# A depthwise convolution accumulated in PSUM, one-bank PSUM tiles in the frequency stage, and TensorE in written order

## The chip, the cores and the metric

The kernel runs on one core of a Trainium2 chip. The metric is device time in microseconds (us) for one execution, the median of several; the profile is of one execution. TensorE is called PE in the profile (its weight loads PEld), VectorE DVE, ScalarE ACT, GpSimd POOL, and the DMA queues of SyncE SP. SBUF is the on-chip working memory; PSUM is the memory that TensorE writes to, eight banks of 512 f32 values in each of 128 partitions.

## The reference

Eight images of 128 x 128 pixels and 64 channels, all f32, go through two layers. The first is criss-cross attention (every pixel attends to its row and its column). The second, called the mixer here, is what the change is about:

```python
h  = _pw(_ln(x, g1, b1), w_te, b_te)                  # 64 -> 128 channels at each pixel
F  = jnp.fft.fft2(h.astype(jnp.complex64), axes=(1, 2))
fr = jnp.concatenate([jnp.real(F), jnp.imag(F)], axis=-1)
fc = jax.nn.gelu(_pw(fr, w_fc, b_fc), approximate=False)   # 256 -> 256
re, im = (fc[..., :HID], fc[..., HID:])
sp = jnp.real(jnp.fft.ifft2(re + 1j * im, axes=(1, 2)))
x1 = x + _pw(sp, w_tp, b_tp)                          # 128 -> 64
h2 = _pw(_ln(x1, g2, b2), w_fe, b_fe)                 # 64 -> 128
d  = lax.conv_general_dilated(h2, w_dw, window_strides=(1, 1), padding='SAME',
         dimension_numbers=('NHWC', 'HWIO', 'NHWC'), feature_group_count=HID) + b_dw   # 3 x 3, depthwise
d  = jax.nn.gelu(d, approximate=False)
return x1 + _pw(d, w_fp, b_fp)                        # 128 -> 64
```

## The kernel before

The attention layer runs first for all eight images and leaves its result in DRAM (`x2`). The mixer then has, for each image, two stages written as Python generators. `fourier(b)` is the frequency stage: Fourier transforms along both axes as matmuls with tables, the 256 x 256 channel mix with its gelu (`fcps`, `gl`), and the inverse (`yps`, `dps`), added to `x1`. `mlp(b)` is what follows: normalisation, expansion to 128 channels, the 3 x 3 convolution, gelu, and the last matmul. The MLP of image b-1 is woven into the frequency stage of image b, piece by piece; the last MLP runs by itself.

PSUM before: `ps_f` two tiles of two banks, `ps_m` and `ps_c` two tiles of one bank each, eight banks in all.

```python
W_STEP, K_STEP, I_STEP = 2.0, 7.0, 5.0
PIECES = 5
LEAD = 6
# ... cut ...
        ps_f = ctx.enter_context(tc.tile_pool(name="m_psf", bufs=2, space=PSUM))
        ps_m = ctx.enter_context(tc.tile_pool(name="m_psm", bufs=2, space=PSUM))
        ps_c = ctx.enter_context(tc.tile_pool(name="m_psc", bufs=2, space=PSUM))
# ... cut: fourier, one of 8 steps of the first transform ...
                aps = ps_f.tile([P, 8, P], F32, tag="fc", name="aps")
                for c in range(8):
                    nc.tensor.matmul(aps[:, c, :], lhsT=xn[:, c0 + c, :], rhs=fwd, start=True, stop=True)
                nc.scalar.copy(at[:, :, c0 : c0 + 8], aps.rearrange("p c k -> p k c"))
                yield W_STEP
# ... cut: the channel mix of one group of four frequencies ...
                    for half in range(2):
                        ps = ps_f.tile([P, 2, 512], F32, tag="fc", name="fcps")
                        cols = slice(half * HID, half * HID + HID)
                        for sgn, w in enumerate((wplus, wminus)):
                            mean = gg[0] == 0
                            nc.tensor.matmul(ps[:, sgn, 0:n], lhsT=w[:, cols], rhs=fv, start=True, stop=not mean)
# ... cut ...
                        nc.scalar.activation(gl[:, :, 0:n], ps[:, :, 0:n], AF.Gelu, bias=bfc[:, half : half + 1])
                        nc.gpsimd.tensor_tensor(
                            gl[:, 0, 0:n], gl[:, 0, 0:n], gl[:, 1, 0:n], ALU.add if half == 0 else ALU.subtract
                        )
# ... cut: the end of the inverse transform ...
        def inverse_w(xs, c0, ys):
            dps = ps_f.tile([P, 8, P], F32, tag="fc", name="dps")
            for g in range(2):
                nc.tensor.matmul(
                    dps[:, 4 * g : 4 * g + 4, :].rearrange("p c h -> p (c h)"), lhsT=idw,
                    rhs=ys[:, 4 * g : 4 * g + 4, :].rearrange("p c h -> p (c h)"), start=True, stop=True,
                )
            for s in range(2):
                xv = xs[s][:, :, c0 : c0 + 8]
                nc.vector.tensor_tensor(xv, dps[:, :, 64 * s : 64 * s + 64].rearrange("p c h -> p h c"), xv, ALU.add)
```

The MLP works on 16 chunks `k` of 8 rows. `normed` (POOL) scales the rows (`xc`), `transposed` brings channels to the partitions (`tpn` on PE, `xtn` on ACT), `expand` makes `h2` (two `hp` matmuls on the two halves of the partitions, and ACT), `taps` is the convolution, `gelu`, `shrink` the last matmul (`op`) and `store` the addition and the DMA:

```python
            def expand(k):
                # ... cut: h2, its borders (POOL memsets), two rows taken over from the chunk before ...
                hps = [ps_c.tile([P, 4, P], F32, tag="mc", name="hp") for _ in range(2)]
                for s in range(2):
                    half = slice(64 * s, 64 * s + 64)
                    nc.tensor.matmul(
                        hps[s].rearrange("p j w -> p (j w)"), lhsT=wfe[half, :],
                        rhs=xt[half, :, :].rearrange("p j w -> p (j w)"), start=True, stop=True,
                    )
                # ... cut: two ACT instructions, hps to h2 ...

            def taps(k, lo, hi):
                i0, i1 = span(k)
                if lo == 0:
                    accs[k] = p2.tile([P, CH + 1, P], F32, tag="acc", name="acc")
                av = accs[k][:, 0 : i1 - i0, :]
                for t in range(lo, hi):
                    src = h2s[k][:, i0 + t // 3 : i1 + t // 3, t % 3 : t % 3 + P]
                    if t == 0:
                        nc.scalar.activation(av, src, AF.Identity, bias=bdw, scale=wdw[:, 0:1])
                    else:
                        nc.vector.scalar_tensor_tensor(
                            out=av, in0=src, scalar=wdw[:, t : t + 1], in1=av, op0=ALU.mult, op1=ALU.add
                        )

            def gelu(k):
                i0, i1 = span(k)
                av = accs[k][:, 0 : i1 - i0, :]
                nc.scalar.activation(av, av, AF.Gelu)
            # ... cut ...
            for k in range(n_ch):
                if k > 0:
                    gelu(k - 1)
                if k + 1 < n_ch:
                    transposed(k + 1)
                if k == 4:
                    statistics(1)
                taps(k, 1, 3)
                yield
                held = shrink(k - 1, 0) if k > 0 else None
                taps(k, 3, 5)
                yield
                if held:
                    store(*held)
                taps(k, 5, 6)
                yield
                if k + 1 < n_ch:
                    expand(k + 1)
                if k + 2 < n_ch:
                    normed(k + 2)
                taps(k, 6, 8)
                yield
                if k + 1 < n_ch:
                    taps(k + 1, 0, 1)
                taps(k, 8, 9)
                yield
```

In the attention layer four engines keep the order in which the program is written. In the mixer the compile-time scheduler orders every engine's instructions itself, before the program ever runs.

## Time and profile before

| | us |
|---|---|
| median of 3 runs | 3831.16 (3825.0 to 3836.74) |
| span of the profiled execution | 3833.7 |

| engine | busy us | share of the span | instructions |
|---|---|---|---|
| PE | 3370.7 | 88% | 33046 |
| PE weight loads | 2387.3 | 62% | 33046 |
| DVE | 2676.3 | 70% | 4432 |
| ACT | 1741.7 | 45% | 2341 |
| POOL | 1607.0 | 42% | 1347 |

An f32 matmul appears as two records. In the slices of the page each digit is the busy share of a fortieth of the span in tenths, and the PEclk row is the clock that TensorE was granted, in tenths of full speed. In a row of a group stand the line, the engine, the operation, output and inputs by the program's names, shapes and the number of instructions; then busy us and mean ns of one; then how long the engine stood idle just before them and who ended that wait. A line of the waits has who waited for whom, the us in total, the number of times and the longest. Busy time counts overlapping records once.

### The profile page before, as it was taken

The numbers are of one execution on the slowest core, as the hardware profiler recorded it, in microseconds if no ns is written. First come the engines' busy times: TensorE is split into PE (matmuls) and PEld (weight loads), VectorE is DVE, ScalarE is ACT, GpSimd is POOL, SyncE is SP. The second block draws the span as 40 slices with busy tenths as digits, with TensorE's granted clock in tenths as the row PEclk, the third lists the DMA queues.
The fourth block names the chain that finished last, engine by engine and source line by source line (L and its number), as shares of the span: only waits on it lengthen the run. The fifth ranks groups of instructions, "written<-read, shape, count | busy, mean of one in ns | idle before, by whom it ended". The sixth has DMA issues, their size and how long they took to land.

```text
span 3833.7 us, 79138 instructions
## 1 busy us (share of the span) xinstructions
PE 3370.7 (88%) x33046; PEld 2387.3 (62%) x33046; DVE 2676.3 (70%) x4432; ACT 1741.7 (45%) x2341; POOL 1607.0 (42%) x1347
## 2 busy tenths in 40 slices
PE   7989989899998679998998998998998998999454
PEld 4666666666666457666665666666665665666333
DVE  3556565664665500788888987888988988978867
ACT  3544535435353233453553553553553554554222
POOL 0333243332433534356356356356356356253111
PEclk7989889999897889998998998998998998999555
DMA  4534434354342511012112112112112112100000
GB/s 101 128 94 121 109 98 124 93 129 108 91 119 69 170 44 45 6 39 58 37 39 58 37 39 58 37 39 58 37 39 58 37 39 53 37 17 17 12 19 20
DMA packets 505190, 242.94 MB, mean 63 GB/s; under 512 B 417026, under 2 KB 486018, under 8 KB 502786
## 3 DMA queue, kind: packets, MB, share of 16 engines
q1 hardware_dynamic: 504834, 237.90, 23.1%
q8 instruction: 260, 4.26, 0.5%
q14 instruction: 96, 0.79, 0.1%
HBM read 169.13 MB, written 67.63 MB: 62 GB/s over the span
## 4 chain that ended last, share of the span: by engine, by line
PE 52%; DVE 26%; issue 8%; POOL 6%; ACT 4%; DMA 2%; SPq 1%; DVEq 0%; POOLq 0%; ACTq 0%
DVE acc L748 18%; PE e L202 6%; PE op L770 5%; PE fcps L595 5%; PE hp L724 4%; PE zp L265 3%; PE yps L655 3%; PE dps L663 3%; PE yps L649 3%; PE sp L289 3%; PE pq L183 3%; PE zp L278 3%; POOL xn L542 2%; PE gps L622 2%; DVE negH L211 2%
## 5 line engine op out<-in xcount | busy, mean ns | idle before, releaser
L748 DVE SCALAR_TENSOR_TENSOR acc<-h,wdw,acc 128x1024 f32<-128x1024 f32 (+2 forms) x1024 | 1612.1, 1594 | 151.5 <-ACT acc L746 131.2
L602 POOL TENSOR_TENSOR gl<-gl 128x512 f32<-128x512 f32 (+2 forms) x272 | 487.1, 1796 | 454.0 <-ACT gl L601 453.9
L770 PE MATMUL op<-wfp,acc 128*128 128x64 f32 x2048 | 292.0, 304 | 163.7 <-ACT acc L755 162.8
L770 PEld LDWEIGHTS op<-wfp,acc 128*128 128x128 f32 x2048 | 278.2, 218 | 187.9 <-ACT acc L755 180.0
L601 ACT ACTIVATE gl<-fcps,bfc 128x1024 f32<-128x1024 f32 (+2 forms) x272 | 292.5, 1077 | 190.7 <-PE fcps L595 180.9
L765 POOL TENSOR_TENSOR ot<-x,bfp 128x512 f32<-128x512 f32 (+1 forms) x144 | 226.2, 1576 | 358.9 <-DMA out_dram<-ot 321.8
L243 ACT ACTIVATE att<-e 128x1024 f32<-128x1024 f32 x256 | 248.3, 1022 | 242.9 <-PE e L202 242.8
L339 POOL TENSOR_TENSOR yo<-yo,xb 128x512 f32<-128x512 f32 x128 | 161.0, 1280 | 430.4 <-issue 296.3
L245 POOL TENSOR_SCALAR_AFFINE_SELECT att<-att 128x1024 f32<-128x1024 f32 x128 | 136.8, 1093 | 419.6 <-ACT att L243 419.6
L729 ACT ACTIVATE h<-hp,bfe 128x512 f32<-128x512 f32 x256 | 171.4, 688 | 291.3 <-PE hp L724 291.1
L595 PE MATMUL fcps<-f,wplus 128*128 128x512 f32 (+2 forms) x544 | 293.7, 622 | 0.0
L622 PEld LDWEIGHTS gps<-wtp,gl 128*128 128x128 f32 x2016 | 246.0, 193 | 57.7 <-issue 55.2
L595 PE MATMUL fcps<-f,wminus 128*128 128x512 f32 (+2 forms) x544 | 275.9, 589 | 0.0
L669 DVE TENSOR_TENSOR x<-dps,x 128x512 f32<-128x512 f32 x128 | 86.2, 683 | 265.2 <-PE dps L663 265.2
L542 POOL TENSOR_TENSOR xn<-xl,scale 128x512 f32<-128x512 f32 x128 | 238.4, 1873 | 57.1 <-DMA xl<-x 56.9
L724 PE MATMUL hp<-xtn,wfe 64*128 64x512 f32 x512 | 243.6, 739 | 21.1 <-DVE ot L774 19.8
L755 ACT ACTIVATE acc<-acc 128x1024 f32<-128x1024 f32 (+2 forms) x128 | 135.4, 1058 | 258.6 <-DVE acc L748 258.6
L202 PE MATMUL e<-qkH 8*128 8x128 f32 (+1 forms) x4096 | 199.7, 316 | 54.4 <-DVE negH L211 50.3
L694 POOL TENSOR_TENSOR xc<-x,scale 128x512 f32<-128x512 f32 x128 | 189.1, 1482 | 129.2 <-PE tpn L703 88.2
L622 PE MATMUL gps<-wtp,gl 128*128 128x64 f32 x2016 | 241.1, 273 | 0.9 <-POOL gl L602 0.9
L202 PEld LDWEIGHTS e<-qkH 8*128 8x128 f32 (+1 forms) x4096 | 164.3, 212 | 122.1 <-DVE negH L211 60.0
L202 PEld LDWEIGHTS e<-qkW 8*128 8x128 f32 (+1 forms) x4096 | 140.6, 194 | 126.4 <-DVE negW L211 36.0
(138 smaller groups left out, 6389.1 us busy)
## 6 DMA issues: line engine op xcount, KB each, us to landing
xl<-in_x_dram SPq DMA_DIRECT2D x256, 128.0 KB
xh<-in_x_dram SPq DMA_DIRECT2D x64, 512.0 KB
xw<-in_x_dram SPq DMA_DIRECT2D x256, 128.0 KB
x<-yo SPq DMA_DIRECT2D x256, 128.0 KB
xl<-x SPq DMA_DIRECT2D x128, 256.0 KB
x<-x SPq DMA_DIRECT2D x16, 2048.0 KB
out_dram<-ot SPq DMA_DIRECT2D x120, 256.0 KB
qkH<-joint SPq DMA_DIRECT2D x256, 2.0 KB
```

Of the source, the lines that this page charges most:

```text
L202: nc.tensor.matmul(es[q // 2][:, q % 2, i, :], lhsT=qk[part, lhs, 4 * (r % 2) + i, :], rhs=qk[part, rhs, 4 * (r % 2) + i, :], start=True, ...
L243: nc.scalar.activation(att, e.rearrange("p q i w -> p (q i) w"), AF.Exp)
L542: nc.gpsimd.tensor_tensor(xn[:, :, h : h + NORM_ROWS], xl.rearrange("p h c -> p c h"), scale1[:, b, h : h + NORM_ROWS].unsqueeze(1).to_bro ...
L595: nc.tensor.matmul(ps[:, sgn, 0:n], lhsT=w[:, cols], rhs=fv, start=True, stop=not mean)
L601: nc.scalar.activation(gl[:, :, 0:n], ps[:, :, 0:n], AF.Gelu, bias=bfc[:, half : half + 1])
L602: nc.gpsimd.tensor_tensor(gl[:, 0, 0:n], gl[:, 0, 0:n], gl[:, 1, 0:n], ALU.add if half == 0 else ALU.subtract)
L622: nc.tensor.matmul(gps[:, j, t, :], lhsT=src[:, 0, j * P : j * P + P], rhs=wtp, start=True, stop=True)
L694: nc.gpsimd.tensor_tensor(xc, rows, scale[:, k * CH : k * CH + CH].unsqueeze(2).to_broadcast([P, CH, C]), ALU.mult)
L724: nc.tensor.matmul(hps[s].rearrange("p j w -> p (j w)"), lhsT=wfe[half, :], rhs=xt[half, :, :].rearrange("p j w -> p (j w)"), start=True, ...
L748: nc.vector.scalar_tensor_tensor(out=av, in0=src, scalar=wdw[:, t : t + 1], in1=av, op0=ALU.mult, op1=ALU.add)
L765: nc.gpsimd.tensor_tensor(ot[:, o : o + m, :], rows, bfp.unsqueeze(1).to_broadcast([P, m, C]), ALU.add)
L770: nc.tensor.matmul(op[:, i, :], lhsT=accs[k][:, a + i, :], rhs=wfp, start=True, stop=True)
```

## The change

Five things are changed together, all in the mixer:

- The convolution's sum `acc` moves from SBUF to PSUM (`ps_a`, two tiles of one bank), in parts of at most four rows; the gelu reads PSUM and writes a new SBUF tile `gd`. The aim is to take the sum's traffic out of SBUF, and with a part per bank to let one part's first tap or gelu run beside the other part's taps.
- That needs two banks, so `ps_f` shrinks to two tiles of one bank: `aps`, `fcps` and `dps` are cut into halves, each with its own evacuation.
- TensorE keeps the written order in the mixer too; the other engines are still ordered by the scheduler.
- The MLP's pieces are put into another order: `shrink` and `store` come later in the chunk, and the second half's statistics are spread over four chunks.
- The step weights that weave MLP pieces into the frequency stage follow the halved `aps` step.

```diff
@@ -35,7 +35,7 @@
 CH = 8
 NORM_ROWS = 8
 
-W_STEP, K_STEP, I_STEP = 2.0, 7.0, 5.0
+W_STEP, K_STEP, I_STEP = 1.0, 7.0, 5.0
 PIECES = 5
 LEAD = 6
 
@@ -441,6 +441,7 @@
         ps_f = ctx.enter_context(tc.tile_pool(name="m_psf", bufs=2, space=PSUM))
         ps_m = ctx.enter_context(tc.tile_pool(name="m_psm", bufs=2, space=PSUM))
         ps_c = ctx.enter_context(tc.tile_pool(name="m_psc", bufs=2, space=PSUM))
+        ps_a = ctx.enter_context(tc.tile_pool(name="m_psa", bufs=2, space=PSUM))
 
         ident = const.tile([P, P], F32, tag="ident", name="m_ident")
         make_identity(nc, ident)
@@ -552,11 +553,11 @@
             im = images[b]
             xn = im["xn"]
             at = big.tile([P, P, C], F32, tag="big", name="at")
-            for c0 in range(0, C, 8):
-                aps = ps_f.tile([P, 8, P], F32, tag="fc", name="aps")
-                for c in range(8):
+            for c0 in range(0, C, 4):
+                aps = ps_f.tile([P, 4, P], F32, tag="fc", name="aps")
+                for c in range(4):
                     nc.tensor.matmul(aps[:, c, :], lhsT=xn[:, c0 + c, :], rhs=fwd, start=True, stop=True)
-                nc.scalar.copy(at[:, :, c0 : c0 + 8], aps.rearrange("p c k -> p k c"))
+                nc.scalar.copy(at[:, :, c0 : c0 + 4], aps.rearrange("p c k -> p k c"))
                 yield W_STEP
             gt = big.tile([P, C, 2, 64], F32, tag="big", name="gt")
             pend_fc, pend_tp = None, None
@@ -588,17 +589,17 @@
                     fv = f.rearrange("p k h -> p (k h)")[:, 0:n]
                     gs = []
                     for half in range(2):
-                        ps = ps_f.tile([P, 2, 512], F32, tag="fc", name="fcps")
+                        gl = p2.tile([P, 2, 512], F32, tag="gl%d" % half, name="gl")
                         cols = slice(half * HID, half * HID + HID)
                         for sgn, w in enumerate((wplus, wminus)):
+                            ps = ps_f.tile([P, 512], F32, tag="fc", name="fcps")
                             mean = gg[0] == 0
-                            nc.tensor.matmul(ps[:, sgn, 0:n], lhsT=w[:, cols], rhs=fv, start=True, stop=not mean)
+                            nc.tensor.matmul(ps[:, 0:n], lhsT=w[:, cols], rhs=fv, start=True, stop=not mean)
                             if mean:
                                 nc.tensor.matmul(
-                                    ps[:, sgn, 0:1], lhsT=dc[:, cols], rhs=ident[0:1, 0:1], start=False, stop=True
+                                    ps[:, 0:1], lhsT=dc[:, cols], rhs=ident[0:1, 0:1], start=False, stop=True
                                 )
-                        gl = p2.tile([P, 2, 512], F32, tag="gl%d" % half, name="gl")
-                        nc.scalar.activation(gl[:, :, 0:n], ps[:, :, 0:n], AF.Gelu, bias=bfc[:, half : half + 1])
+                            nc.scalar.activation(gl[:, sgn, 0:n], ps[:, 0:n], AF.Gelu, bias=bfc[:, half : half + 1])
                         nc.gpsimd.tensor_tensor(
                             gl[:, 0, 0:n], gl[:, 0, 0:n], gl[:, 1, 0:n], ALU.add if half == 0 else ALU.subtract
                         )
@@ -658,15 +659,15 @@
             return ys
 
         def inverse_w(xs, c0, ys):
-            dps = ps_f.tile([P, 8, P], F32, tag="fc", name="dps")
             for g in range(2):
+                dps = ps_f.tile([P, 4, P], F32, tag="fc", name="dps")
                 nc.tensor.matmul(
-                    dps[:, 4 * g : 4 * g + 4, :].rearrange("p c h -> p (c h)"), lhsT=idw,
+                    dps.rearrange("p c h -> p (c h)"), lhsT=idw,
                     rhs=ys[:, 4 * g : 4 * g + 4, :].rearrange("p c h -> p (c h)"), start=True, stop=True,
                 )
-            for s in range(2):
-                xv = xs[s][:, :, c0 : c0 + 8]
-                nc.vector.tensor_tensor(xv, dps[:, :, 64 * s : 64 * s + 64].rearrange("p c h -> p h c"), xv, ALU.add)
+                for s in range(2):
+                    xv = xs[s][:, :, c0 + 4 * g : c0 + 4 * g + 4]
+                    nc.vector.tensor_tensor(xv, dps[:, :, 64 * s : 64 * s + 64].rearrange("p c h -> p h c"), xv, ALU.add)
 
         def lines(xs, lo, hi):
 
@@ -680,13 +681,15 @@
             xs = images.pop(b)["x1"]
             n_ch = P // CH
             scale = p2.tile([P, P], F32, tag="scale2", name="scale2")
-            xts, h2s, accs = {}, {}, {}
-
-            def statistics(s):
-                stats = p2.tile([P, 64, 6], F32, tag="stats", name="stats", bufs=1)
-                for r in range(64):
-                    nc.vector.bn_stats(stats[:, r, :], xs[s][:, r, :])
-                deviation(nc, p2, stats, epsc, scale[:, 64 * s : 64 * s + 64])
+            xts, h2s, accs, gls, sts = {}, {}, {}, {}, {}
+
+            def statistics(s, lo, hi):
+                if lo == 0:
+                    sts[s] = p2.tile([P, 64, 6], F32, tag="stats", name="stats", bufs=1)
+                for r in range(lo, hi):
+                    nc.vector.bn_stats(sts[s][:, r, :], xs[s][:, r, :])
+                if hi == 64:
+                    deviation(nc, p2, sts[s], epsc, scale[:, 64 * s : 64 * s + 64])
 
             def normed(k):
                 xc = p2.tile([P, CH, C], F32, tag="xc", name="xc")
@@ -735,11 +738,16 @@
 
                 return (1 if k == 0 else 0), (CH + 1 if k == n_ch - 1 else CH)
 
-            def taps(k, lo, hi):
+            def part(k, u):
+
                 i0, i1 = span(k)
+                return max(i0, 4 * u), min(i1, 4 * u + 4)
+
+            def taps(k, u, lo, hi):
+                i0, i1 = part(k, u)
                 if lo == 0:
-                    accs[k] = p2.tile([P, CH + 1, P], F32, tag="acc", name="acc")
-                av = accs[k][:, 0 : i1 - i0, :]
+                    accs[k, u] = ps_a.tile([P, 4, P], F32, tag="acc", name="acc")
+                av = accs[k, u][:, 0 : i1 - i0, :]
                 for t in range(lo, hi):
                     src = h2s[k][:, i0 + t // 3 : i1 + t // 3, t % 3 : t % 3 + P]
                     if t == 0:
@@ -749,10 +757,11 @@
                             out=av, in0=src, scalar=wdw[:, t : t + 1], in1=av, op0=ALU.mult, op1=ALU.add
                         )
 
-            def gelu(k):
-                i0, i1 = span(k)
-                av = accs[k][:, 0 : i1 - i0, :]
-                nc.scalar.activation(av, av, AF.Gelu)
+            def gelu(k, u):
+                i0, i1 = part(k, u)
+                if u == 0:
+                    gls[k] = p2.tile([P, CH + 1, P], F32, tag="gd", name="gd")
+                nc.scalar.activation(gls[k][:, i0 : i1, :], accs.pop((k, u))[:, 0 : i1 - i0, :], AF.Gelu)
 
             def shrink(k, a):
 
@@ -767,14 +776,14 @@
                     )
                 op = ps_c.tile([P, CH, C], F32, tag="mc", name="op")
                 for i in range(n):
-                    nc.tensor.matmul(op[:, i, :], lhsT=accs[k][:, a + i, :], rhs=wfp, start=True, stop=True)
+                    nc.tensor.matmul(op[:, i, :], lhsT=gls[k][:, i0 + a + i, :], rhs=wfp, start=True, stop=True)
                 return r0, n, ot, op
 
             def store(r0, n, ot, op):
                 nc.vector.tensor_tensor(ot[:, 0:n, :], op[:, 0:n, :], ot[:, 0:n, :], ALU.add)
                 nc.sync.dma_start(out=out[b, r0 : r0 + n, :, :].rearrange("h w c -> w h c"), in_=ot[:, 0:n, :])
 
-            statistics(0)
+            statistics(0, 0, 64)
             normed(0)
             normed(1)
             for _ in range(LEAD):
@@ -783,34 +792,39 @@
             yield
             expand(0)
             yield
-            taps(0, 0, 1)
+            taps(0, 0, 0, 1)
             for k in range(n_ch):
                 if k > 0:
-                    gelu(k - 1)
+                    gelu(k - 1, 1)
+                taps(k, 1, 0, 1)
                 if k + 1 < n_ch:
                     transposed(k + 1)
-                if k == 4:
-                    statistics(1)
-                taps(k, 1, 3)
+                taps(k, 0, 1, 4)
                 yield
-                held = shrink(k - 1, 0) if k > 0 else None
-                taps(k, 3, 5)
-                yield
-                if held:
-                    store(*held)
-                taps(k, 5, 6)
+                if 1 <= k <= 4:
+                    statistics(1, 16 * k - 16, 16 * k)
+                taps(k, 0, 4, 8)
                 yield
                 if k + 1 < n_ch:
                     expand(k + 1)
                 if k + 2 < n_ch:
                     normed(k + 2)
-                taps(k, 6, 8)
+                taps(k, 0, 8, 9)
+                gelu(k, 0)
+                taps(k, 1, 1, 3)
                 yield
+                held = shrink(k - 1, 0) if k > 0 else None
+                taps(k, 1, 3, 6)
+                yield
+                if held:
+                    store(*held)
                 if k + 1 < n_ch:
-                    taps(k + 1, 0, 1)
-                taps(k, 8, 9)
+                    taps(k + 1, 0, 0, 1)
+                taps(k, 1, 6, 9)
                 yield
-            gelu(n_ch - 1)
+            gelu(n_ch - 1, 1)
+            taps(n_ch - 1, 2, 0, 9)
+            gelu(n_ch - 1, 2)
             for a in (0, CH):
                 store(*shrink(n_ch - 1, a))
             yield
@@ -818,7 +832,7 @@
 
 
         pieces = LEAD + 3 + PIECES * (P // CH)
-        work = W_STEP * 8 + K_STEP * (len(groups) + 2) + I_STEP * 9
+        work = W_STEP * 16 + K_STEP * (len(groups) + 2) + I_STEP * 9
         for _ in load_norm(0):
             pass
         for b in range(NB + 1):
@@ -851,7 +865,8 @@
     E = mybir.EngineType
     with tc.manual_schedule(engines={E.PE, E.DVE, E.Activation, E.Pool}):
         attention(tc, nc, x, w_q, b_q, w_k, b_k, w_v, b_v, gamma, x2, scale1)
-    mixer(tc, nc, x2, scale1, tbl, prm, out)
+    with tc.manual_schedule(engines={E.PE}):
+        mixer(tc, nc, x2, scale1, tbl, prm, out)
 
 
 _INS = [
```

## Prediction

> **What bounds the kernel now.** I read the slices first, then one window per image of the second layer (the mixer), then in one such window the groups, the waits and the order in time. Slices:
>
> ```profile
> PE   7989989899998679998998998998998998999454
> DVE  3556565664665500788888987888988988978867
> PEclk7989889999897889998998998998998998999555
> ```
>
> The first 13 slices are the attention layer, which the change leaves alone: the mixer's first matmul `aps` starts at 1364 us. Behind it every image shows the same picture until PE and its clock fall to 4 and 5 in the last three slices. One window for image 0 (frequency stage alone), one for a middle image (frequency stage with the MLP of the image before woven in), the last such image, and the last MLP, which runs by itself:
>
> ```profile
> 1364.00:1552.00 188.00, 186.43 (x1336) 137.39 (x1337) 9.02 (x14) 74.67 (x93) 65.18 (x50) 0.99 0.09 25
> 2422.00:2712.00 290.00, 268.87 (x1719) 189.75 (x1718) 246.52 (x300) 145.01 (x193) 151.95 (x118) 0.92 0.16 44
> 3292.00:3565.00 273.00, 256.24 (x1701) 181.08 (x1699) 234.74 (x300) 143.88 (x192) 112.20 (x102) 0.97 0.08 20
> 3565.00:3834.00 269.00, 122.78 (x402) 86.09 (x402) 195.80 (x287) 75.23 (x100) 41.95 (x65) 0.50 0.08 17
> ```
>
> The columns are length, then busy time of PE, its weight loads, DVE, ACT and POOL, then the granted clock. Image 0 is pure TensorE: 186 of 188 us busy at clock 0.99. Six middle images start 289 us apart (`aps` from 1552 to 3288 us), at PE 268 and clock 0.92 to 0.94, with DVE at 246. The last MLP takes 269 us with PE busy for less than half of it. So 1364 + 188 + 6 x 289 + 277 + 269 = 3832 us is the whole time, and the change touches everything but the first term.
>
> What does the MLP cost TensorE if nothing waits? In the chain of waits sixteen `op` records take 1.73 us, and an image has 256: 27.7 us. In order of time:
>
> ```profile
> 2529.44 1.12 PE L724 MATMUL hp<-xtn,wfe 64*128 64x512 f32 x2
> 2531.65 1.12 PE L724 MATMUL hp<-xtn,wfe 64*128 64x512 f32 x2 [0.45 <-DVE ot L774]
> 2549.74 1.13 PE L724 MATMUL hp<-xtn,wfe 64*128 64x512 f32 x4
> ```
>
> Two `hp` matmuls issued together (four records) take 1.13 us, but apart they take 1.12 us each. Kept together, 16 pairs an image start 1.06 us apart: 17 us. Transposes: 16 times four records at about 0.53 us: 8.5 us. Sum 53 us, so 188 + 53 = 241 us of TensorE work against 289: some 48 us an image are waits, the lower clock that follows them, and split pairs.
>
> The DVE and POOL rows say where the waits are from (middle image 2417 to 2708 us, and for POOL also image 0, where DVE has nothing to do):
>
> ```profile
> L748 DVE SCALAR_TENSOR_TENSOR acc<-h,wdw,acc 128x1024 f32<-128x1024 f32 x112 | 187.5, 1691 | 16.9 <-ACT acc L746 14.4
> L669 DVE TENSOR_TENSOR x<-dps,x 128x512 f32<-128x512 f32 x17 | 11.5, 682 | 6.3 <-PE dps L663 6.3
> L602 POOL TENSOR_TENSOR gl<-gl 128x512 f32<-128x512 f32 x30 | 55.8, 1865 | 51.4 <-ACT gl L601 51.4
> ...
> L602 POOL TENSOR_TENSOR gl<-gl 128x512 f32<-128x512 f32 x30 | 38.0, 1268 | 91.2 <-ACT gl L601 91.2
> ```
>
> The same POOL addition takes 1.27 us beside an idle DVE and 1.87 us beside the taps. The 1024-element tap takes 1.27 us when undisturbed and 1.69 us in the mean. The row that reads `dps` out of PSUM never stretches: 675 to 695 ns over all 128.
>
> TensorE's longest waits in that image, and then DVE's longest in the last MLP:
>
> ```profile
> PE tpn L703 <- ACT h L729: 5.8, 4, 2.2
> PE gps L612 <- POOL gl L602: 4.2, 1, 4.2
> PE op L770 <- ACT acc L755: 3.6, 1, 3.6
> ...
> DVE ot L774 <- PE op L770: 58.0, 16, 6.7
> ```
>
> The first three are MLP work or POOL being late. The last is an order fault: the final addition stands in DVE's queue right where its matmuls are only being issued, so DVE stands idle 58 us.
>
> [...] the taps (two SBUF inputs) stretch from 1.27 to 2.2 us, the `dps` additions (one SBUF, one PSUM) stay at 0.68. [...] No row here writes PSUM from DVE. [...] 0.99 in image 0, 0.92 with 21 us of waits, 0.50 in the last MLP.
>
> **The change part by part.** *Taps in PSUM.* 128 x 8 x 128 elements per image stay 8 passes over 16,384 elements, but in 33 pieces of at most four rows, 264 instructions for 128. Each now reads one operand from SBUF and one from PSUM. From these starts I take the spacing:
>
> ```profile
> 2399.70 0.68 DVE L669 TENSOR_TENSOR x<-dps,x 128x512 f32<-128x512 f32 x1
> 2400.30 0.68 DVE L774 TENSOR_TENSOR ot<-op,ot 128x512 f32<-128x512 f32 x1
> 2400.90 2.59 DVE L748 SCALAR_TENSOR_TENSOR acc<-h,wdw,acc 128x1024 f32<-128x1024 f32 x2
> ```
>
> 0.60 us per 512 elements, against 1.19 for 1024 in SBUF undisturbed: splitting is nearly free. [...] Taps: 8 x 17.07 + 264 x 0.07 = 155 us. Statistics 128 x 0.127 = 16; `dps` additions, now 32 of 256 elements at 0.34, 11; stores 10; deviations 3. DVE 195 us an image instead of 246. POOL without blocking: `gl` 41, `xn` 16 x 1.50 = 24, `ot` 16 x 1.29 = 21, `xc` 16 x 1.06 = 17, memsets 4: 107 instead of 152.
>
> *Written order on TensorE.* All 128 `hp` pairs stand together; 49 of the 128 are split now: 49 x 1.05 = 51 us over the run, 6 an image. `op` is issued three pieces after the gelu it needs, its addition one piece after that, in the middle of taps: that removes the 58 us at the end. The price: TensorE no longer steps aside. At an image's end the order is two `dps`, nine `op`, and only then the next `aps`; before, 34 `aps` stood ahead of the last `op`. Those nine need DVE's last adds (1.3 us), the remaining taps (about 5) and a gelu (0.6), so 7 us of idle TensorE per image, and about 2 more at half clock.
>
> *Single banks.* `fcps`, 68 of 0.86 us an image, has two single banks instead of two double ones. A gelu of 512 lasts 0.68 us, so it just keeps up, and falls behind when ACT has one of the MLP's 0.6 us instructions between two gelus. I choose 0.1 us in the mean: 7 us an image. ACT itself grows by half-size instructions (two 0.68 for one 1.11) from 145 to some 165 us, no bound.
>
> *Sum.* Per middle image 241 + 9 + 7 = 257, and I add 8 for the inverse steps, where DVE (2.3 MLP pieces of 2.1 us and 1.35 of additions, 6.2 us) and TensorE (5.3 + 1.4 = 6.7 us) are so level that either's lateness is felt: 265. The last woven image has no loading beside it: 260. Last MLP: DVE's 195 less 11, plus 16 us to start (statistics to first tap) and 10 to end: 210. Image 0: 189. 1364 + 189 + 6 x 265 + 260 + 210 = 3613 us.
>
> **The rivals.** (1) A DVE write to PSUM, or reading back what was just written there, costs more than the `dps` row shows. For: no row of the kernel does it. Against: consecutive taps in SBUF, equally dependent, start 1.20 us apart against 1.19 before another instruction. At 0.72 us a tap DVE has 224 us, the inverse steps become DVE's, an image about 272, the end 235: near 3690. At double cost, 1.1 us, DVE alone would be 325 us and the kernel slower, near 4100. (2) TensorE in written order stalls as much as the scheduler's order did, and the clock stays at 0.92. Then only the pairs and the last MLP gain: 3832 - 60 - 45 = about 3730. For: ACT is in order too, and one late gelu blocks what stands behind it. Against: waits here come from late DVE and POOL work, and both get 45 us of slack per image. (3) TensorE saturates at 0.97 or more and the stalls vanish: 250 an image, near 3510.
>
> **Range and chances.** The middle image is the uncertain term, 252 to 278, seven times; the end adds 20 either way. That gives 3520 to 3710, with the longer side from rival 1 and 2. Slower than 3755 (2% less) needs both rivals mild or the first badly: 6%. Slower than now by 2% is only the first at double cost: 2%.
>
> **What would show it.** Taps of 512 elements at 0.68 us and no two populations; POOL's `gl` at 1.27 us in the middle images; images 265 us apart with PE clock 0.94 to 0.97; `hp` always in fours; DVE's wait for `op` in the last MLP gone; a wait of `op` for the last gelu at each image's end. I am wrong if the taps last over 0.8 us, or if `fcps` waits for ACT by more than 15 us an image.

## The result and the profile after

| | before | after |
|---|---|---|
| median, us (runs on the same chip) | 3828.1 (4) | 3698.3 (4) |
| ratio | | 0.966, 95% interval 0.962 to 0.970 |

The kernel is 3.4% faster. The prediction was 3613 us with a range of 3520 to 3710: the direction and the range held, but the gain is 130 us where I had said 215.

The slices of the changed kernel, as those shown of before:

```profile
PE   7989999899999939999899899899899899899654
DVE  3566574655656510377877877877877877877988
PEclk7999898898998869999999999999999999999755
```

The clock row is the change at a glance: nearly all nines in the mixer. DVE stands lower in every image and higher at the end. The windows, cut at the same events as before (image 0, a middle image, the last woven one, the last MLP; length, then PE, weight loads, DVE, ACT, POOL, clock):

```profile
1358.00:1550.00 192.00, 189.92 (x1336) 134.75 (x1336) 11.34 (x30) 84.62 (x135) 65.22 (x50) 0.99 0.08 25
2370.00:2643.00 273.00, 249.87 (x1722) 177.73 (x1722) 216.67 (x452) 156.91 (x267) 104.85 (x118) 0.97 0.17 47
3193.00:3465.00 272.00, 249.57 (x1712) 177.58 (x1712) 212.89 (x440) 156.53 (x266) 81.20 (x100) 0.97 0.08 20
3465.00:3699.00 234.00, 112.60 (x394) 77.75 (x394) 205.68 (x425) 78.77 (x135) 39.99 (x66) 0.50 0.09 20
```

A middle image went from 289 to 273 us, the last MLP from 269 to 234, and image 0 grew by 4. In a middle image TensorE's busy time fell by 19 us, to 250, while its idle time stayed at 21 to 23 us. So the gain there is not a smaller sum of waits: it is the pairs of `hp` (from start to start 28 us an image before, 17.5 now) and the clock, 0.97 for 0.92. The idle time is cut up differently. Before, TensorE had six waits of 1.9 to 4.2 us in a middle image, spread over it, and half of the clock for some 44 us; now it has two, of 4.1 and 3.8 us, both at the image's end, and half of the clock for 17 us around them. One stretch at half clock before, behind a wait of 2.2 us, and then the 256 us between two image ends now:

```profile
2465.10:2471.90 6.80, 6.45 (x24) 3.84 (x25) 6.76 (x6) 3.61 (x6) 2.54 (x2) 0.50 0.15 34
```

```profile
2375.00:2631.00 256.00, 240.11 (x1679) 168.35 (x1678) 200.93 (x383) 153.81 (x261) 104.38 (x115) 1.00 0.15 40
```

POOL fell from 152 to 105 us. The groups of DVE and POOL in the middle image:

```profile
L756 DVE SCALAR_TENSOR_TENSOR acc<-h,wdw,acc 128x512 f32<-128x512 f32 x248 | 172.9, 749 | 16.3 <-ACT acc L754 14.2
```

```profile
L603 POOL TENSOR_TENSOR gl<-gl 128x512 f32<-128x512 f32 x30 | 38.1, 1270 | 54.8 <-ACT gl L602 54.8
```

POOL's addition is back at the 1.27 us that it had beside an idle DVE, and a tap is 749 ns in the mean. What TensorE waits for in this image:

```profile
PE op L779 <- ACT gd L764: 9.2, 3, 4.1
PE op L779 <- ACT h L732: 6.2, 8, 0.8
PE hp L727 <- ACT xtn L710: 5.3, 6, 1.4
PE fcps L597 <- ACT gl L602: 1.2, 4, 0.8
```

The first line is the stall at the image's end that the prediction named. The second and third it did not: they are MLP matmuls that wait for the ACT copy of the matmul issued just before them.

### The profile page after: what moved, and what is told of

Read it like the earlier page. It is cut to its first block, busy times and chain, and to the rows that moved or that the text cites. A ratio compares the mean times of both kernels' runs of the same rounds, so it can differ in the third digit from the quotient of the medians.

```text
span 3698.8 us, 81162 instructions
## 1 busy us (share of the span) xinstructions
PE 3249.9 (88%) x33046; PEld 2304.9 (62%) x33046; DVE 2488.0 (67%) x5648; ACT 1841.9 (50%) x2937; POOL 1295.3 (35%) x1347
## 5 line engine op out<-in xcount | busy, mean ns | idle before, releaser
L756 DVE SCALAR_TENSOR_TENSOR acc<-h,wdw,acc 128x512 f32<-128x512 f32 (+2 forms) x2112 | 1429.1, 733 | 137.4 <-ACT acc L754 119.9
L603 POOL TENSOR_TENSOR gl<-gl 128x512 f32<-128x512 f32 (+2 forms) x272 | 332.1, 1222 | 479.4 <-ACT gl L602 479.2
L779 PE MATMUL op<-wfp,gd 128*128 128x64 f32 x2048 | 298.9, 306 | 202.0 <-ACT h L732 123.7
L779 PEld LDWEIGHTS op<-wfp,gd 128*128 128x128 f32 x2048 | 282.8, 219 | 289.3 <-ACT h L732 193.7
L602 ACT ACTIVATE gl<-fcps,bfc 128x512 f32<-128x512 f32 (+2 forms) x544 | 360.8, 669 | 116.3 <-PE fcps L597 81.9
L774 POOL TENSOR_TENSOR ot<-x,bfp 128x512 f32<-128x512 f32 (+1 forms) x144 | 167.4, 1167 | 519.2 <-DMA out_dram<-ot 447.9
L670 DVE TENSOR_TENSOR x<-dps,x 128x256 f32<-128x256 f32 x256 | 103.3, 418 | 278.3 <-PE dps L664 277.5
L764 ACT ACTIVATE gd<-acc 128x512 f32<-128x512 f32 (+2 forms) x264 | 153.8, 582 | 216.6 <-DVE acc L756 215.6
L783 DVE TENSOR_TENSOR ot<-op,ot 128x512 f32<-128x512 f32 (+2 forms) x136 | 89.3, 657 | 221.1 <-PE op L779 167.3
L754 ACT ACTIVATE acc<-h,bdw,wdw 128x512 f32<-128x512 f32 (+2 forms) x264 | 202.9, 772 | 9.0 <-ACT h L732 0.4
```

The lines of the kernel that those rows point to most:

```text
L602: nc.scalar.activation(gl[:, sgn, 0:n], ps[:, 0:n], AF.Gelu, bias=bfc[:, half : half + 1])
L603: nc.gpsimd.tensor_tensor(gl[:, 0, 0:n], gl[:, 0, 0:n], gl[:, 1, 0:n], ALU.add if half == 0 else ALU.subtract)
L756: nc.vector.scalar_tensor_tensor(out=av, in0=src, scalar=wdw[:, t : t + 1], in1=av, op0=ALU.mult, op1=ALU.add)
L774: nc.gpsimd.tensor_tensor(ot[:, o : o + m, :], rows, bfp.unsqueeze(1).to_broadcast([P, m, C]), ALU.add)
L779: nc.tensor.matmul(op[:, i, :], lhsT=gls[k][:, i0 + a + i, :], rhs=wfp, start=True, stop=True)
```

## The experiments

Two theories. **A**: most of the gain is from the sum leaving SBUF, so that DVE and POOL no longer block each other. **B**: most of it is from TensorE's written order. A later one, **C**, is on what the written order still loses. All ratios are to the kernel before, run on the same chip. e1 to e7 ran on one chip, e8 to e11 on a second and e12 on a third; across these groups the ratios are to be compared, not the times.

| run | what it is | median us | ratio (95%) |
|---|---|---|---|
| the changed kernel | all five parts | 3698.3 | 0.966 (0.962 to 0.970) |
| e1 | TensorE ordered by the scheduler | 3656.5 | 0.956 (0.954 to 0.958) |
| e2 | sum in SBUF, same parts and order | 4032.8 | 1.055 (1.053 to 1.057) |
| e3 | e2, frequency stage with two-bank tiles | 3999.0 | 1.047 (1.045 to 1.049) |
| e4 | the kernel before, written order only | 3823.6 | 1.000 (0.999 to 1.002) |
| e5 | last `op` of an image issued later | 3695.6 | 0.965 (0.962 to 0.968) |
| e6 | e5, MLP pieces woven in more finely | 3650.4 | 0.953 (0.949 to 0.956) |
| e7 | first and last tap in other memories | 3686.0 | 0.964 (0.960 to 0.968) |
| e8 | e6, fewer pieces in the inverse steps | 3630.6 | 0.952 (0.950 to 0.954) |
| e9 | scheduler's order, finer pieces, e8's weights | 3679.0 | 0.964 (0.961 to 0.966) |
| e10 | sum in PSUM, scheduler's order, old pieces | 3718.9 | 0.975 (0.972 to 0.977) |
| e11 | e2, TensorE ordered by the scheduler | 3972.0 | 1.040 (1.038 to 1.043) |
| e12 | e8, `op` one piece later | 3643.5 | 0.952 (0.948 to 0.956) |

### e1: the written order undone

```diff
-    with tc.manual_schedule(engines={E.PE}):
-        mixer(tc, nc, x2, scale1, tbl, prm, out)
+    mixer(tc, nc, x2, scale1, tbl, prm, out)
```

> The changed kernel with one part undone: TensorE's order in the mixer is left to the scheduler again. Theory A (most of the gain is from the convolution's sum leaving SBUF, so that DVE and POOL no longer block each other): most of the gain stays, 3720 to 3760 us; POOL's gl stays at 1.2 us and the taps at 0.66 us apart; hp pairs are split again (some 6 us an image). Theory B (most of the gain is from the written order on TensorE): the gain goes, 3790 us or more, with images 285 us apart and the TensorE clock back at 0.93.

Neither: the gain does not stay or go, it grows by 42 us. Written order, which is part of the change, costs 1%. A middle image takes 267 us instead of 273. Its window, and TensorE's waits in it:

```profile
2347.00:2614.00 267.00, 255.19 (x1722) 181.12 (x1723) 214.99 (x452) 157.32 (x269) 104.17 (x118) 0.97 0.17 48
```

```profile
PE op L779 <- ACT gd L764: 5.2, 2, 4.1
...
PE op L779 <- ACT h L732: 1.1, 2, 0.8
```

Beside the changed kernel's lines: `op` behind `h` is 1.1 us instead of 6.2, and `hp` behind `xtn` is gone. TensorE is 5 us busier and idles 12 us instead of 23. The `hp` pairs, expected to be split again, mostly stay together: one of sixteen is split in this image, 8 of 128 in the whole run (49 in the kernel before).

### e2, e3, e11: the sum back in SBUF

```diff
-                    accs[k, u] = ps_a.tile([P, 4, P], F32, tag="acc", name="acc")
+                    if u == 0:
+                        gls[k] = p2.tile([P, CH + 1, P], F32, tag="gd", name="gd")
+                    accs[k, u] = gls[k][:, i0:i1, :]
```

> The changed kernel with the convolution's sum back in SBUF, in the same parts of four rows and with the same pieces and order (the first tap and the gelu work in place in gd; ps_a stays empty). Theory A: the two populations of taps come back (about 0.65 and 1.6 us for 512 elements), POOL's gl goes from 1.22 to 1.8 us, DVE gets to 250 us or more an image, and the kernel to 3820 us or more, perhaps above the kernel before, as TensorE in written order waits for it. Theory B: within 40 us of the changed kernel, 3700 to 3740 us.

Theory A, and more strongly than it said: 335 us above the changed kernel, and 5.5% above the kernel before. The middle image (they take 325 us in the mean), and its taps and POOL addition:

```profile
2199.00:2526.00 327.00, 279.49 (x1721) 200.71 (x1721) 258.90 (x451) 159.87 (x267) 158.72 (x118) 0.87 0.14 39
```

```profile
L758 DVE SCALAR_TENSOR_TENSOR gd<-h,wdw,gd 128x512 f32<-128x512 f32 x248 | 214.4, 925 | 1.3 <-ACT gd L756 1.1
```

```profile
L603 POOL TENSOR_TENSOR gl<-gl 128x512 f32<-128x512 f32 x30 | 81.1, 2710 | 36.4 <-ACT gl L602 36.3
```

The same number of taps, on the same shapes, in the same order: 925 ns for 749, and POOL's addition 2.71 us for 1.27 in the mean. That mean hides what happens. Over the whole run (number, then shortest, median and longest in ns), first the kernel before, then e2:

```profile
L602 POOL TENSOR_TENSOR gl<-gl x272: 713/1893/2357, 1389.5 to 3489.2; 128x512 f32<-128x512 f32 x120, 128x384 f32<-128x384 f32 x8, 128x256 f32<-128x256 f32 x8
```

```profile
L603 POOL TENSOR_TENSOR gl<-gl x272: 715/1271/12982, 1380.4 to 3726.3; 128x512 f32<-128x512 f32 x120, 128x384 f32<-128x384 f32 x8, 128x256 f32<-128x256 f32 x8
```

Most additions are as fast as undisturbed, and a few last up to 13 us. One of them, and what DVE did meanwhile (start, length):

```profile
2229.04 14.20 DVE L758 SCALAR_TENSOR_TENSOR gd<-h,wdw,gd 128x512 f32<-128x512 f32 x20
```

```profile
2230.08 12.62 POOL L603 TENSOR_TENSOR gl<-gl 128x512 f32<-128x512 f32 x1 [7.33 <-ACT gl L602]
```

One addition stands through a whole row of short taps; beside the kernel before's long taps none lasted over 2.4 us. POOL's busy time in all is not much more than in the kernel before, 159 us an image for 152, but single results come very late, and TensorE's `gps` waits 12.6 us an image for POOL where it waited 5.2. The last MLP, with little POOL work beside it, takes 230 us here, no more than in the changed kernel: the loss is all in the woven images.

e3 gives the four idle banks back to the frequency stage (`aps`, `fcps`, `dps` as in the kernel before):

> As the run with the sum in SBUF, and the four banks go back to the frequency stage (aps, fcps, dps in tiles of two banks with one evacuation each, as before). My prediction gave single banks 7 us an image: then this is some 50 us below the run with the sum in SBUF. The rival, that one bank at a time keeps up and costs nothing: the same time within 10 us. Image 0, which has no MLP beside it, shows it by itself: 188 us with two banks, 192 with one.

34 us less than e2: an image 321 us instead of 325, and image 0 188 us. Single banks cost about 4 us an image, between the two. This is measured with the sum in SBUF; with the sum in PSUM there are no banks left to try it.

e11 is e2 without the written order:

> The run with the sum in SBUF in parts, with TensorE's order left to the scheduler: tells whether the 4033 us of that run is contention by itself or contention that TensorE's written order makes worse. Contention by itself (as many short taps, each of which can block or be blocked by a POOL instruction): 3980 us or more. Made worse by the written order: 3900 us or less.

3972 us, just under the line that I had drawn for contention by itself and far above the other. Taking the sum out of SBUF is worth 315 us in the scheduler's order (e11 to e1) and 335 in the written one. It must not be read as the gain over the kernel before: twice as many short taps keep DVE busy for 267 us an image in e11, 246 in the kernel before, and the late POOL additions (in e11 up to 13.2 us) are not found there.

### e4: the kernel before in written order

```diff
-    mixer(tc, nc, x2, scale1, tbl, prm, out)
+    with tc.manual_schedule(engines={E.PE}):
+        mixer(tc, nc, x2, scale1, tbl, prm, out)
```

> The kernel before with one part of the change: TensorE in written order in the mixer, all else as it was (sum in SBUF, two-bank tiles, old pieces). Theory A: no gain, 3830 to 3900 us: hp pairs stay together, but TensorE stands at op and hp until blocked DVE work is done. Theory B: at least half of the gain, 3770 us or less. In both the 58 us for which DVE waited for op in the last MLP should mostly stay, as it comes from where the pieces stand and from the order that the scheduler gives DVE.

No difference, as A has it. In a middle image TensorE is busy 7 us less (pairs together) and waits as much more. DVE's wait in the last MLP, to the tenth what it was:

```profile
DVE ot L774 <- PE op L770: 58.0, 16, 6.7
```

### e10: old pieces, with the sum in PSUM

```diff
+            def both(k, lo, hi):
+                for t in range(lo, hi):
+                    for u in range(2):
+                        taps(k, u, t, t + 1)
             # the loop over chunks as in the kernel before, with both() for taps(), but:
-                    gelu(k - 1)
+                    gelu(k - 1, 0)
+                    gelu(k - 1, 1)
+                both(k, 0, 1)
```

> The changed kernel without its written order and without its new order of pieces: sum in PSUM, single banks, TensorE ordered by the scheduler, the MLP's pieces as before, except that the first tap of a chunk comes right after the gelu of the chunk before, as its bank is free only then. Tells what the new order of pieces is for. Expected: POOL's gl at 1.25 us and the taps 0.66 us apart as in the changed kernel, but DVE waits for gelu and first tap at every chunk (2.5 us, 16 times, 40 us an image), so 280 us an image, and the last MLP at 265 us as before instead of 234: 3750 to 3790 us. Rival (the pieces' order is of no account, PSUM is all): 3660 to 3690 us.

3719 us: between the two. DVE's longest waits in a middle image of 276 us, and in the last MLP:

```profile
DVE acc L756 <- ACT acc L754: 51.5, 21, 10.2
```

```profile
DVE acc L756 <- ACT acc L754: 14.2, 16, 1.4
DVE ot L783 <- PE op L779: 4.7, 3, 1.8
```

The wait for the first tap at every chunk is there (34 us in e1, with the new pieces). The new order of pieces is worth 62 us (e10 to e1; 72 by the ratios, as the two ran on different chips). That this wait is what costs them is not shown. A middle image takes 9 us more than in e1, and TensorE's `hp`, first in e10 and then in e1, have most of it, because 8 of 16 pairs are split here and one there:

```profile
L727 PE MATMUL hp<-xtn,wfe 64*128 64x512 f32 x64 | 27.0, 641 | 0.0
```

```profile
L727 PE MATMUL hp<-xtn,wfe 64*128 64x512 f32 x64 | 20.1, 672 | 0.0
```

So the old pieces may cost by what the scheduler does to TensorE's order as much as by DVE's waits.

The runs make a chain from the kernel before to the changed one: with the sum in PSUM, and the parts and single banks that go with it, 0.975 (e10); with the new pieces 0.956 (e1); with the written order 0.966. The sum's new place is the largest single gain, as theory A has it, but not by much.

I was wrong on the last MLP: it takes 232 us here too. The old 58 us wait falls to 19 us or less without the new pieces being needed, in every run in which the sum is cut into parts and the gelu or the first tap stands apart from it (e1, e2, e3, e10), and stays with the kernel before's whole sums (e4). Which of these two moves DVE's addition in the scheduler's order was not separated.

### e7: what makes a tap cost 0.66 us

The taps of the changed kernel in order of time (start, length):

```profile
2603.56 0.75 DVE L756 SCALAR_TENSOR_TENSOR acc<-h,wdw,acc 128x512 f32<-128x512 f32 x1
2604.22 0.42 DVE L670 TENSOR_TENSOR x<-dps,x 128x256 f32<-128x256 f32 x1
2604.55 0.74 DVE L756 SCALAR_TENSOR_TENSOR acc<-h,wdw,acc 128x512 f32<-128x512 f32 x1
2605.21 0.42 DVE L670 TENSOR_TENSOR x<-dps,x 128x256 f32<-128x256 f32 x1
```

A tap takes 0.66 us until the next start, an addition of half its size 0.33. I had predicted 0.60 and 0.34.

```diff
-                        nc.scalar.activation(av, src, AF.Identity, bias=bdw, scale=wdw[:, 0:1])
+                        nc.scalar.activation(sv, src, AF.Identity, bias=bdw, scale=wdw[:, 0:1])
-                            out=av, in0=src, scalar=wdw[:, t : t + 1], in1=av, op0=ALU.mult, op1=ALU.add
+                            out=sv if t == 8 else av, in0=src, scalar=wdw[:, t : t + 1],
+                            in1=sv if t == 1 else av, op0=ALU.mult, op1=ALU.add
```

(`sv` is the part's place in `gd`, in SBUF.)

> The changed kernel with two of nine taps changed in where the sum lies: the first tap goes to SBUF (ACT), the second tap reads the sum from SBUF and writes PSUM, six go from PSUM to PSUM, the last reads PSUM and writes SBUF, where the gelu works in place. It tells what makes a tap start 0.658 us apart instead of the 0.605 I predicted from additions that read PSUM and write SBUF. If the write to PSUM costs it: taps that read PSUM and write SBUF are 0.605 apart, and those that read SBUF and write PSUM 0.65. If reading back PSUM costs it: 0.658 and 0.62. If it is the operation with its scalar operand, all are 0.65. The second tap alone has two SBUF inputs and so alone should show the second population, at 1.2 us and more. In total 3700 to 3740 us.

Number of instructions, then shortest, median and longest in ns, by where the sum is read and written (`gd` is SBUF, `acc` PSUM); the first line is from the view of the tile `acc`, the others from that of `gd`:

```profile
L758 DVE SCALAR_TENSOR_TENSOR acc<-h,wdw,acc x1584: 343/747/755, 1577.3 to 3686.9; 128x512 f32<-128x512 f32 x190, 128x128 f32<-128x128 f32 x6, 128x384 f32<-128x384 f32 x2
```

```profile
L758 DVE SCALAR_TENSOR_TENSOR acc<-h,wdw,gd x264: 354/755/2009, 1576.6 to 3681.6; 128x512 f32<-128x512 f32 x124, 128x384 f32<-128x384 f32 x4, 128x128 f32<-128x128 f32 x4
L758 DVE SCALAR_TENSOR_TENSOR gd<-h,wdw,acc x264: 336/743/748, 1584.8 to 3687.3; 128x512 f32<-128x512 f32 x124, 128x384 f32<-128x384 f32 x4, 128x128 f32<-128x128 f32 x4
```

All three medians are within 12 ns. In the kernel before an addition that reads PSUM and writes SBUF, 0.60 us from start to start, has a median length of 0.68 us; a tap that does the same has 0.74, and the other taps 0.75. The fourth form, from SBUF to SBUF, is in e2's last MLP:

```profile
3988.34 10.67 DVE L758 SCALAR_TENSOR_TENSOR gd<-h,wdw,gd 128x512 f32<-128x512 f32 x16
3998.94 0.68 DVE L783 TENSOR_TENSOR ot<-op,ot 128x512 f32<-128x512 f32 x1
```

Sixteen in 10.60 us, 0.66 each again: it is the operation, not the memory. The total of 3686 us cannot be told from the changed kernel's; 3700 to 3740 had been expected. And only the row with two SBUF inputs has a long tail, 2.0 us; 264 of them run in the same kernel beside 1848 without one that exceeds 0.755 us. That is the contention in one view, within one kernel and so within one order.

### e5, e6: what the written order loses

e5 moves the last two groups of `op` and their stores behind nine `aps` steps of the next image:

```diff
-            for a in (0, CH):
-                store(*shrink(n_ch - 1, a))
+            late.append(finish)          # the same two lines; run at once for the last image
...
-            for _ in range(LEAD):
+            for n in range(LEAD):
+                if n == 4 and late:
+                    late.pop()()
                 yield
```

> The changed kernel with one move: the last two groups of op matmuls of an image (nine) and their stores are issued not at the image's end but after nine of the sixteen aps steps of the next image. My prediction gave the stall there 9 us an image (7 idle, 2 at half clock). If that is right: seven woven images each 8 to 10 us shorter, 3635 us. Rival (the wait is only put off, because the MLP that follows has to catch up on DVE anyway): under 3 us an image, 3680 us or more.

The rival was right: 3 us in all, less than the runs scatter. TensorE's waits in a middle image (276 us):

```profile
PE op L779 <- ACT h L732: 6.2, 8, 0.8
PE aps L559 <- DVE x L670: 5.5, 1, 5.5
PE hp L727 <- ACT xtn L710: 5.1, 6, 1.1
PE tpn L706 <- POOL xc L697: 4.1, 1, 4.1
```

The 9.2 us of `op` behind the gelu are gone, and in their place stand `aps`, which needs the bank that the last `x` addition frees, and `tpn`, which needs the statistics: 9.6 us. At the image's end DVE is behind (in the changed kernel it is busy for 65 of the 75 us of the inverse steps), and TensorE meets it at whichever instruction comes first. (Theory C.)

e6 adds two more places where pieces of the MLP are woven in:

```diff
+K_PARTS = (1.8, 3.4, 1.8)
...
                 tp_next = None
+                yield K_PARTS[0]                  # after fps
...
                     tp_next = (gg, gs)
+                yield K_PARTS[1]                  # after fcps
...
-                yield K_STEP
+                yield K_PARTS[2]                  # after gps
```

> The run with the late op, and the MLP's pieces are woven in after each third of a frequency step (after fps, after fcps, after gps) instead of three or four at once. The changed kernel's TensorE waits in the K steps are op behind the ACT copy of hp just before it, and hp behind the ACT copy of tpn just before it, 10 us an image: they arise where pieces that depend on each other are issued back to back. If so: 5 to 8 us an image less than the run with the late op, 3590 us. Rival (ACT is what is late, whatever stands between): within 10 us of the run with the late op; fcps may then even wait longer, as ACT work is spread among the gelus.

45 us less than e5, 6.5 us a woven image, as expected; the 3590 us had also counted on e5's gain, which did not come. In a middle image of 269 us:

```profile
PE aps L560 <- DVE x L673: 5.5, 1, 5.5
PE tpn L709 <- POOL xc L700: 4.1, 1, 4.1
PE op L782 <- ACT h L735: 3.9, 5, 0.8
PE fcps L599 <- ACT gl L604: 2.1, 5, 0.8
PE hp L730 <- ACT xtn L713: 1.8, 2, 1.2
```

`hp` behind `xtn` and `op` behind `h` fell from 11.3 to 5.7 us, `fcps` rose by 1: dependent matmuls issued back to back were most of what written order lost.

### e8, e12, e9: attempts at the rest

```diff
-W_STEP, K_STEP, I_STEP = 1.0, 7.0, 5.0
-K_PARTS = (1.8, 3.4, 1.8)
+W_STEP, K_STEP, I_STEP = 1.0, 7.6, 3.75
+K_PARTS = (1.95, 3.7, 1.95)
```

> The run with the finer pieces, and the weights moved so that fewer MLP pieces fall into the inverse steps (15 of 89 instead of 21) and more into the K steps. In the changed kernel DVE is busy 65 of 75 us in the inverse steps and 18 of 20 in the aps steps after them, but only 134 of 178 in the K steps. Theory C (at the image's end TensorE waits because DVE is behind; moving the op away only moved the wait to the next instruction that needs DVE): the 9.6 us that TensorE waits there (aps for the last x additions 5.5, tpn for xc 4.1) shrink to 5 or less, 4 to 6 us an image, 3610 to 3625 us. Rival (those waits come from the statistics, which can start only after the last addition): within 10 us of the run with the finer pieces.

```profile
PE op L782 <- ACT h L735: 6.0, 2, 5.2
PE fcps L599 <- ACT gl L604: 4.9, 4, 3.3
PE tpn L709 <- POOL xc L700: 2.3, 1, 2.3
...
PE aps L560 <- DVE x L673: 1.3, 2, 1.1
```

The mechanism of C holds, 3.6 us at the image's end for 9.6, but `op` and `fcps` took back 5: the ratio, 0.952, cannot be told from e6's 0.953. e12 issues `op` one piece later and its addition two:

```diff
-                held = shrink(k - 1, 0) if k > 0 else None
                 taps(k, 1, 3, 6)
                 yield
-                if held:
-                    store(*held)
+                if k > 0:
+                    held.append(shrink(k - 1, 0))
 # ... cut: in the next chunk, after its first piece ...
+                while held:
+                    store(*held.pop())
```

> The run with the pieces moved forward, and op goes one piece later in the chunk and its addition two, so that a third of a frequency step stands between hp and op, and between tpn and hp. In the run before it TensorE waits 6 to 8 us an image at op for the ACT copies of hp, and 3 to 5 at fcps. If dependent MLP matmuls too close together are what the written order loses, the wait at op falls below 2 us and the kernel gains 4 to 7 us an image: 3585 to 3605 us. Rival (the time of an image is by now set by DVE's and TensorE's work together, and a wait removed comes back elsewhere): 3620 us or more.

The rival again: 0.952, and one wait of `op` for `h`, 5.2 us long, is still there. What makes that one instance was not found. e9 combines the scheduler's order (e1) with e8's weights and finer pieces:

> The changed kernel with TensorE's order left to the scheduler, and with the finer pieces and the moved weights (the last op stays where the changed kernel has it). If the scheduler's order and the finer pieces gain by the same thing (keeping dependent MLP instructions apart), they do not add: 3640 to 3660 us. If they gain by different things: below 3620 us.

Neither: 3679 us, 23 above e1 (29 by the ratios). DVE now waits 38 us an image for first taps (34 in e1), and a `dps` waits 4.6 us for DVE. The two remedies do not add, which fits their acting on the same waits, but a loss was not expected. One thing that goes with it: the scheduler splits 28 of the 128 `hp` pairs here, 8 in e1. At 1.06 us for a pair and 1.05 for each half, as in the kernel before, 20 more splits would be some 21 us of TensorE (an estimate); that they are the cause was not tested.

## Why the prediction was right, and where it was off

- **Contention goes.** Right: POOL 105 us an image (107 predicted), one population of taps (none over 0.758 us, median 0.750). e2 and e7 show that it is the sum's place that does it.
- **A tap's cost.** The form of the sum was right and a term mis-sized: 0.07 us fixed per tap, taken from the `dps` additions because they read PSUM (0.601 us in the kernel before, less 4 x 0.133). The changed kernel's taps of 128, 384 and 512 elements start 0.258, 0.525 and 0.659 us before the next tap (medians): 0.133 us for 128 elements, which is the 17.07 us of a pass over 16,384, and some 0.125 fixed; e7 and e2 show that this belongs to the operation and not to the memory. I could have read it: the kernel before's undisturbed taps of 896 and 1152 elements start 1.06 and 1.33 us apart, which leaves 0.13 fixed in each. 264 x 0.055 = 14 us of DVE an image: 209 instead of 195 (217 in the busy row). Rival 1 in its mild form gave 3690 us, near the measured time, but not by its own step: a tap costs 0.66 and not 0.72 us, and PSUM is not why.
- **`hp` pairs.** Right: always together, 1.13 us.
- **Written order takes away the 58 us in the last MLP.** Wrong. e4 has the order and the wait of 58 us; e1 and e10 do without the order and have 19 and 5 us. The cut sum does it, or the gelu's and first tap's new place.
- **Written order in the woven images.** The step "waits here come from late DVE and POOL work, and both get slack" failed: half of the waits now are TensorE-ACT-TensorE chains issued back to back, 11.5 us an image, that the scheduler used to pull apart. The order is a net loss of 42 us (e1); I had it as a gain. Rival 2 was half right: TensorE idles as long as before, 23 us an image for 21, but not at the old clock (0.97 for 0.92). What it rested on, that ACT works in order, shows in the kernel before: ACT stood for 5.95 us before a gelu that waited for a tap, and a `ys` copy whose matmuls had ended at 2648.1 us came behind it at 2652.97.
- **The stall at an image's end.** Named rightly and somewhat too small: 9.2 us of idle TensorE for 7, and half clock for 17 us around it. Its cause was half right: removing it gained nothing (e5), as DVE is behind there anyway.
- **Single banks.** 7 us an image predicted for gelus that fall behind. `fcps` waits 1.2 us for them in the changed kernel; e2 against e3 gives 4 us an image in all.
- **The last MLP.** 234 us for 210: 14 of the 24 are the tap's fixed cost. DVE's waits for `op`, which I had put at nothing, are 19 us of that stage; part of them is made up elsewhere in it.
- **The pieces.** Their new order had a term only in the last MLP, where it is not needed (e10). It is worth some 60 us all the same, in the woven images.
- **Sum.** 273 instead of 265 for a middle image and 272 instead of 260 for the last woven one; with the last MLP's 24 us this is nearly all of the 85 us. That the middle image came so close is in part luck. The chains of 11.5 us were in no term; against that, `fcps` takes 1.2 us of the 7 allowed, and the 8 us for the inverse steps do not appear: DVE is busy for 65 of 75 us there, but apart from the stall at the end TensorE waits 1.5 us in them.

## What to carry to other kernels

Where two SBUF inputs on VectorE run beside GpSimd, try the running sum in PSUM: here it relieved both engines (GpSimd's addition from 1.87 to 1.27 us, and no 512-element tap over 0.758 us, where the 1024-element ones took 1.27 us undisturbed and up to 2.58). Look at the longest GpSimd instruction and not only at the mean: beside a row of short taps it was ten times the median (12.98 us for 1.27, e2). Take an instruction's fixed cost from its own operation's rows, even if they are of another memory or size (0.125 us for the tap, 0.07 for the addition). Written order on TensorE kept pairs together here (28 us of `hp` an image before, 17.5 after) but issues each dependent matmul right behind its producer's copy (waits of 11.5 us an image): weave in one piece at a time (0.953 here), or leave the order to a scheduler (0.956, which cannot be told from it), and before removing a stall, ask which engine is behind, as the next instruction that needs it may stall instead (in e5 for 9.6 us, after 9.2).

## What I had not expected of the hardware

- Beside a row of VectorE taps of 512 elements, each with two SBUF inputs, one GpSimd addition lasted 12.6 us (e2; up to 13.2 us in e11), where it takes 1.27 us beside an idle VectorE. Beside taps of 1024 elements the longest was 2.4 us. Why it lasts so long beside the short ones was not tested; the order of the pieces differs too.
- A VectorE `scalar_tensor_tensor` of 512 f32 elements cost the same in all four places of its sum: 0.66 us from start to start from PSUM to PSUM (the changed kernel) and from SBUF to SBUF (e2), and median lengths of 755, 747 and 743 ns from SBUF to PSUM, PSUM to PSUM and PSUM to SBUF (e7). A plain addition of the same size from PSUM starts 0.60 us before the next instruction.
- The same idle time, 21 and 23 us an image, came with clocks of 0.92 and 0.97. The four waits of 1.9 to 2.2 us in a middle image of the kernel before were each followed by half of the clock for 3.4 to 6.8 us; in the changed kernel 19 waits of up to 1.4 us left it at 1.00 for 256 us.
